# The last routed layer of a transformer block in three float32r products instead of float32 matmuls

## Chip, cores, metric

The kernel runs on one core of a Trainium2 chip. A core has TensorE (PE, matrix products; PEld is its weight load), VectorE (DVE), ScalarE (ACT), GpSimd (POOL) and SyncE (SP), which issues the transfers. The metric is the device time of one execution in microseconds. Each engine works off its own queue in order; engines wait for each other by semaphores.

## The reference, cut to what matters

```python
x = x + attn_a(layernorm(x))      # x is (8, 512, 256) float32
x = x + ffn(layernorm(x))
x = x + attn_b(layernorm(x))      # gated linear attention, then a SwiGLU
x = x + ffn(layernorm(x))         # the layer that changes; same weights as the second line

def ffn(x):                       # 4096 tokens of 256 channels, 16 blocks of 64 hidden units
    prob = softmax(x @ router_w.T + router_b)
    mask = the 4 largest of the 16 blocks, token by token
    h = relu((x @ w1.T + b1) * mask_of_the_block)      # 1024 hidden units
    return h @ w2.T + b2
```

The router chooses four blocks by their rank, so the layers before it are computed in float32; the kernel computes all hidden units of all tokens and masks.

## The kernel before, in words

The residual stream stays in SBUF (`xres`, batches by slices of 128 positions). After the first attention, the rest is done for four slices k of 8 x 128 = 1024 tokens: a routed layer, linear attention (`gla`), a SwiGLU and a second routed layer. The order of the work is written out by hand at the end of `block_kernel` (lines 1411 to 1450): `between` (L904) runs a list of matmul units and, between them, steps of generators (`pieces`) that make the next stages ready on the other engines. A scheduling layer then orders each engine's queue, within what the code's tiles and buffers allow; a tile that reuses a buffer waits for the buffer's last readers.

`route(k, key)` (L990) normalizes a slice, turns it with TensorE into channels by tokens (`xnT`, two halves g of 512 tokens), adds the bias b2 to `xres` on GpSimd (L1000), computes the router and writes the mask. The mask goes to DRAM (`md`) and comes back spread over 64 partitions each (`mk`, four transfers of 256 KB, L1070), all on SP's queue. For the last layer, slices 0 and 1 are routed during swiglu(2) and swiglu(3), slices 2 and 3 during the last layer's own slices 0 and 1.

`routed_ffn(k, key, last)` (L1113) computes a half of 512 tokens at a time. For each of the 8 rows of 128 hidden units, two float32 matmuls with 512 columns (L1118) go into a PSUM bank, ScalarE (L1126) or, in the last layer for odd rows, VectorE (L1124) adds b1 and applies ReLU, and VectorE multiplies by the mask (L1127). Then `down` (L1083) takes two batches at a time: 2 x 8 matmuls of 256 columns (L1092), with 128 tokens of h as the loaded operand, and VectorE adds the result to `xres` (L1103, at the very end L1100). In the last layer each `xres` of 256 KB is then stored. `swiglu(k)` (L1140) has the same shape with other weights.

PSUM has four banks for hidden units (`ps_h`, L886), two for outputs (`ps_y`) and two for the routing and attention pieces (`ps_l`).

Weights: the routed layers' w1 and w2, the linear attention's projections (`q_w`, `q_wo` and smaller ones, L852 to L882) and the SwiGLU's weights (L883 to L885) are all loaded in this order on SP's queue, ahead of the out-projection (`out_projection`, L972, from `outC`), in the pool `wpool`. After the out-projection the pool that held `outC` is closed (L1412) and a pool `rest` opened in its space for the linear attention's tiles.

The type `HALF` is float32r, another reading of the same 32 bits. The first attention already uses it: queries are split in an upper and a lower part (`qh`, `ql`), and each part is a float32r matmul (L582, L608). The changed functions and what calls them:

Of the kernel before, what the change touches and what calls it, by code (L numbers as in the profile page):

```python
# [33 lines left out]
LN_EPS = 1e-5  # L34
RMS_EPS = 1e-6
REPL = -(2.0**127)
SENT = -(2.0**126)


@with_exitstack  # L40
def block_kernel(ctx: ExitStack, tc: tile.TileContext, t: dict, out: bass.AP):
    nc = tc.nc
# [6 lines left out]
    out_v = out.rearrange("b (k p) d -> p b k d", p=P)  # L49
# [57 lines left out]
    with ExitStack() as outer:  # L107
# [5 lines left out]
        def bank(name):  # L113
            return ps_e.tile([P, 512], F32, tag="e", name=name)
# [68 lines left out]
        with ExitStack() as inner:  # L183
# [7 lines left out]
                out=head_of, in_=head_of, compare_op=ALU.is_ge, fill=0.0,  # L191
# [3 lines left out]
                out=head_of, in_=head_of, compare_op=ALU.is_ge, fill=0.0,  # L195
# [456 lines left out]
            def top_queries():  # L652
# [28 lines left out]
            first = front(0, lambda name: next(both)(name), True)  # L681
# [56 lines left out]
            for n in range(len(steps) + LAG + 1):  # L738
# [3 lines left out]
                batch, i = divmod(n - LEAD, 16)  # L742
# [76 lines left out]
        wpool = ctx.enter_context(tc.tile_pool(name="wpool", bufs=1, side="right"))  # L819
# [3 lines left out]
        for h in range(2):  # L823
            nc.sync.dma_start(
                out=rw[:, :, h, bass.ts(h, NBLK)],
                in_=t["f_router_wT"].rearrange("(c p) e -> p c e", p=P),
            )
        rb = load_rows(wpool, "rb", t["L0_ffn_router_b"], nc.sync)
        w1 = load_chunked(wpool, "w1", t["f_w1T"], nc.sync)
        b1 = load(wpool, "b1", t["f_b1c"], nc.sync)  # L830
        w2 = load_chunked(wpool, "w2", t["f_w2T"], nc.sync)
        b2 = load_rows(wpool, "b2", t["L0_ffn_b2"], nc.sync)

        with tc.tile_pool(name="a_tail", bufs=2) as tail:
# [5 lines left out]
            last = outC[5][0:1, 1, 0:1]  # L840
# [8 lines left out]

    G4 = NB // 2  # L850

    q_w = wpool.tile([P, NC2, NC2, 4, P], F32, name="q_w")  # L852
    for i, name in enumerate(("b_wkT", "b_wqT", "b_wvT", "b_wogT")):
        for c in range(NC2):
            nc.sync.dma_start(
                out=q_w[:, c, :, i, :],
                in_=t[name][bass.ts(c, P), :].rearrange("p (m n) -> p m n", n=P),
            )
    q_wo = load_chunked(wpool, "q_wo", t["b_woT"], nc.sync)


    q_wg1 = wpool.tile([P, NC2, 32], F32, name="q_wg1")
    q_wg2 = wpool.tile([P, D], F32, name="q_wg2")
    q_bg1 = wpool.tile([P, 1], F32, name="q_bg1")
    gh = wpool.tile([P, 2 * P], F32, name="gh")
    for w in (q_wg1, q_wg2, q_bg1):
        nc.gpsimd.memset(w, 0.0)
    nc.gpsimd.memset(gh, 1.0)
    nc.sync.dma_start(
        out=q_wg1[:, :, 0:DH], in_=t["b_wg1T"].rearrange("(c p) e -> p c e", p=P)  # L870
    )
    for u in range(G4):
        r = 32 * u + DH
        nc.sync.dma_start(out=q_wg2[32 * u : r, :], in_=t["b_wg2T"])
        nc.sync.dma_start(
            out=q_wg2[r : r + 1, :].rearrange("o (c p) -> o c p", p=P),
            in_=t["b_bg2c"].rearrange("p c -> c p").unsqueeze(0),
        )
        nc.sync.dma_start(out=q_bg1[32 * u : r, :], in_=t["b_bg1c"])
    q_bog = load(wpool, "q_bog", t["b_bogc"], nc.sync)  # L880
    scale1 = load(wpool, "scale1", t["b_scale1c"], nc.sync)
    scale2 = load(wpool, "scale2", t["b_scale2c"], nc.sync)  # L882
    w_gate = load_chunked(wpool, "w_gate", t["b_w_gateT"], nc.sync)  # L883
    w_up = load_chunked(wpool, "w_up", t["b_w_upT"], nc.sync)
    w_down = load_chunked(wpool, "w_down", t["b_w_downT"], nc.sync)  # L885
# [6 lines left out]
    def bank_h(name):  # L892
        return ps_h.tile([P, 512], F32, tag="h", name=name)
# [10 lines left out]
    def between(units, pieces, n):  # L904

        done = 0
        for i, unit in enumerate(units):
            unit()
            while done < n * (i + 1) // len(units):
                next(pieces, None)  # L910
                done += 1
        for _ in pieces:
            pass

    def tokens(k, b, n=2):
        return xres[:, b : b + n, k, :]

    def pairs(y):
        return y.rearrange("p (b d) -> p b d", d=D)
# [67 lines left out]
    ready = {}  # L987
    ROUTE = 10
# [124 lines left out]
    def routed_ffn(k, key, last):  # L1113
        def unit(h, g, f):
            xT, mk = ready[key]
            ps = bank_h("h_ps")
            for c in range(NC2):
                nc.tensor.matmul(  # L1118
                    ps, w1[:, c, bass.ts(f, P)], xT[g][:, c, :],
                    start=(c == 0), stop=(c == NC2 - 1),  # L1120
                )
            hf = hidden()
            if last and f % 2:
                nc.vector.tensor_scalar(hf, ps, b1[:, f : f + 1], 0.0, ALU.add, ALU.max)  # L1124
            else:
                nc.scalar.activation(hf, ps, AF.Relu, bias=b1[:, f : f + 1])  # L1126
            nc.vector.tensor_tensor(hf, hf, mk[g][:, f, :], ALU.mult)  # L1127
            h.append(hf)
            newest[0] = hf[0:1, 0:1]

        units = []
        for g in range(2):
            h = []
            units += [functools.partial(unit, h, g, f) for f in range(NF)]
            for u in range(2):
                units += down(h, w2, k, g, u, last)
        return units


    def swiglu(k):  # L1140
        def unit(h, pg, g, f, w):
            zT = ready["z", k]
            ps = bank_h("swi_ps")
            for c in range(NC2):
                nc.tensor.matmul(  # L1145
                    ps, w[:, c, bass.ts(f, P)], zT[g][:, c, :],
                    start=(c == 0), stop=(c == NC2 - 1),
                )
            if w is w_gate:
                hf = hidden()  # L1150
                nc.scalar.activation(hf, ps, AF.Silu)  # L1151
# [12 lines left out]
        return units  # L1164
# [5 lines left out]
    def gla(k):  # L1170
# [186 lines left out]
        for b in range(0, NB, 2):  # L1357
            y = bank_l("gla_y")
            for i in range(2):
                for m in range(NC2):  # L1360
                    nc.tensor.matmul(  # L1361
                        y[:, bass.ts(i, D)], oT[:, b // G4, m, bass.ts(b % G4 + i, P)],
                        q_wo[:, m, :],
                        start=(m == 0), stop=(m == NC2 - 1),
                    )
            z = post.tile([P, 2, D], F32, tag="z", name="z", bufs=4)
# [36 lines left out]
    def chain(*gens):  # L1403
        return itertools.chain(*gens)
# [8 lines left out]
    rest = ctx.enter_context(tc.tile_pool(name="rest", bufs=1, reuse_waits="tile"))  # L1413

    bog = wpool.tile([P, NC2, P], F32, name="bog")
# [27 lines left out]
    between(routed_ffn(3, (1, 3), False), chain(g[1], some(g[2], 34)), GLA - 42)  # L1443
    between(swiglu(1), chain(g[2], some(g[3], 24)), GLA - 10)
    between(swiglu(2), chain(g[3], route(0, (2, 0))), GLA - 24 + ROUTE)
    between(swiglu(3), route(1, (2, 1)), ROUTE)
    between(routed_ffn(0, (2, 0), True), route(2, (2, 2)), ROUTE)
    between(routed_ffn(1, (2, 1), True), route(3, (2, 3)), ROUTE)
    for k in (2, 3):
        between(routed_ffn(k, (2, k), True), iter(()), 0)  # L1450


# [47 lines left out]
```

## Time and profile before

| what | us |
|---|---|
| median of three runs (1587.17, 1594.52, 1595.94) | 1594.52 |
| span of the profiled execution, first to last instruction | 1583.6 |
| median of the runs above that span | 10.9 |
| TensorE busy | 1536.1 (97%) |
| VectorE busy | 942.4 (60%) |
| ScalarE busy | 703.6 (44%) |
| GpSimd busy | 454.0 (29%) |

The profile shows one execution; its span lies inside the time that the runs measure. Its page gives the engines' busy times, then the span in 40 slices, the chain of work that ended last, and groups of instructions: line, engine, operation, tile written and tiles read, shape, number, then busy time and mean duration, then the idle time before them and what ended it. The timeline view lists instructions in order of time: start, length, engine, line, operation, tiles, number of them. Busy times of matmuls overlap, since they are pipelined; their rate is read from the distance between starts.

### The profile page before, as it was taken

Reading aid. Unit: us, or ns where it says so; the run is one execution under the profiler, and the core shown is the slowest. Engines: PE = TensorE matmul, PEld = TensorE weight load, DVE = VectorE, ACT = ScalarE, POOL = GpSimd, SP = SyncE. Lnnn points to the kernel's source line nnn. Section 1 sums busy time; section 2 is a strip of 40 time slices with the busy share of each in tenths; the row PEclk is TensorE's granted clock in tenths of the full one; section 3 lists DMA queues with packets and bytes.
Section 4 is the critical chain, followed back from the end, with each engine's and each line's share of the span. In section 5 each row is a group of like instructions: output and inputs, shape, how many; then the busy total and the mean of one; then the engine's idle time right before and its main releaser. Section 6 shows DMA issues by size and latency. Waiting matters only on the chain.

```text
span 1583.6 us, 21546 instructions
## 1 busy us (share of the span) xinstructions
PE 1536.1 (97%) x7982; PEld 858.6 (54%) x7982; DVE 942.4 (60%) x1974; ACT 703.6 (44%) x1290; POOL 454.0 (29%) x547
## 2 busy tenths in 40 slices
PE   6899999999999899999899999999999999999999
PEld 3444444444444466655565556546545655667666
DVE  5888776776788864456834556567176532354332
ACT  4477777677778543532254225332631532211110
POOL 4743352452221241232433223334143310100000
PEclk9899999999999899999999999999999999999999
DMA  5301112112110330100000000000000010001100
GB/s 190 124 26 59 42 46 79 42 42 82 42 42 3 92 102 9 42 1 14 0 1 0 0 25 4 0 0 1 1 1 1 1 28 1 27 28 46 35 27 27
DMA packets 38553, 52.65 MB, mean 33 GB/s; under 512 B 9068, under 2 KB 22580, under 8 KB 38448
## 3 DMA queue, kind: packets, MB, share of 16 engines
q1 hardware_dynamic: 37648, 50.09, 9.8%
q8 instruction: 63, 1.03, 0.3%
q10 hardware_dynamic: 800, 1.18, 0.2%
q14 instruction: 42, 0.34, 0.1%
HBM read 21.24 MB, written 4.33 MB: 16 GB/s over the span
## 4 chain that ended last, share of the span: by engine, by line
PE 74%; DVE 11%; POOL 5%; ACT 4%; issue 3%; DMA 2%; SPq 0%; POOLq 0%; DVEq 0%; ACTq 0%
PE y_ps L1092 16%; PE h_ps L1118 10%; PE s L608 9%; PE swi_ps L1145 8%; PE av L630 7%; PE proj_ps L1231 7%; PE s L582 4%; DVE pr L1264 2%; PE q_ps L440 2%; POOL o L1281 2%; DVE pr L1254 2%; PE k_ps L440 2%; PE gla_y L1361 2%; PE v_ps L507 2%; DVE w L1256 2%
## 5 line engine op out<-in xcount | busy, mean ns | idle before, releaser
L588 DVE TENSOR_REDUCE mx<-s 128x1 f32<-128x512 f32 x512 | 325.3, 684 | 108.8 <-PE s L582 107.7
L615 ACT ACTIVATE e<-s 128x512 f32<-128x512 f32 x512 | 275.9, 600 | 119.5 <-PE s L608 115.0
L1092 PE MATMUL y_ps<-w,h 128*128 128x256 f32 x1024 | 232.9, 383 | 8.7 <-DVE h L1127 8.1
L1118 PE MATMUL h_ps<-xnT,w 128*128 128x512 f32 x512 | 228.2, 594 | 0.0
L1092 PEld LDWEIGHTS y_ps<-w,h 128*128 128x128 f32 x1024 | 193.2, 191 | 47.1 <-DVE h L1127 12.0
L1118 PEld LDWEIGHTS h_ps<-xnT,w 128*128 128x128 f32 x512 | 94.7, 190 | 105.8 <-issue 104.1
L630 PE MATMUL av<-e,va 128*32 128x512 f32 (+1 forms) x1216 | 144.4, 543 | 2.0 <-ACT st L640 2.0
L1126 ACT ACTIVATE h<-h_ps,b 128x512 f32<-128x512 f32 x96 | 65.3, 685 | 176.7 <-PE h_ps L1118 176.7
L1127 DVE TENSOR_TENSOR h<-h,mk 128x512 f32<-128x512 f32 x128 | 94.0, 748 | 80.4 <-ACT h L1126 60.7
L582 PE MATMUL s<-km,qh 32*128 32x512 f32 x512 | 135.6, 501 | 5.8 <-DMA km<-half 4.1
L608 PE MATMUL s<-qh,km 32*128 32x512 f32 x512 | 138.6, 499 | 0.4 <-ACT e L615 0.3
L1103 DVE TENSOR_TENSOR xres<-xres,y_ps 128x512 f32<-128x512 f32 x47 | 32.2, 685 | 154.4 <-PE y_ps L1092 117.2
L1145 PE MATMUL swi_ps<-zT,w_up 128*128 128x512 f32 x256 | 121.7, 594 | 0.2 <-DVE h L1154 0.2
L1145 PE MATMUL swi_ps<-zT,w_gate 128*128 128x512 f32 x256 | 121.4, 593 | 0.0
L1092 PE MATMUL y_ps<-w_down,h 128*128 128x256 f32 x512 | 117.6, 380 | 0.0
L1231 PE MATMUL proj_ps<-q_w,rT 128*128 128x512 f32 x256 | 115.7, 595 | 0.9 <-ACT al L1214 0.4
L608 PE MATMUL s<-ql,km 32*128 32x512 f32 x512 | 111.2, 400 | 0.0
L582 PE MATMUL s<-km,ql 32*128 32x512 f32 x512 | 109.5, 404 | 0.0
L608 PE MATMUL s<-tops,takes 4*128 4x512 f32 x512 | 109.0, 394 | 0.0
L582 PEld LDWEIGHTS s<-km,qh 32*128 32x128 f32 x512 | 54.4, 184 | 96.1 <-DVE mx L588 64.4
L1092 PEld LDWEIGHTS y_ps<-w_down,h 128*128 128x128 f32 x512 | 95.1, 190 | 19.0 <-issue 7.4
L1151 ACT ACTIVATE h<-swi_ps 128x512 f32<-128x512 f32 x64 | 38.1, 595 | 139.7 <-PE swi_ps L1145 139.6
(235 smaller groups left out, 2186.9 us busy)
## 6 DMA issues: line engine op xcount, KB each, us to landing
mk<-md SPq DMA_DIRECT2D x32, 256.0 KB
qh<-half SPq DMA_DIRECT2D x63, 128.0 KB
ql<-half SPq DMA_DIRECT2D x63, 128.0 KB
km<-half SPq DMA_DIRECT2D x63, 128.0 KB
out<-xres SPq DMA_DIRECT2D x15, 256.0 KB
xres<-in_L_attn_a_x SPq DMA_DIRECT2D x7, 512.0 KB
w<-in_f_w1T SPq DMA_DIRECT2D x1, 1024.0 KB
w<-in_f_w2T SPq DMA_DIRECT2D x1, 1024.0 KB
```

What stands on the lines that cost most here:

```text
L440: nc.tensor.matmul(ps, w[:, c, bass.ts(m, P)], x[:, c, :], start=(c == 0), stop=(c == NC2 - 1),)
L582: nc.tensor.matmul(s, (qh, ql)[i].bitcast(HALF)[rows, e, bass.ts(k, P)], km.bitcast(HALF)[rows, e, :], start=(i == 0), stop=(i == 1),)
L588: nc.vector.tensor_reduce(mx[:, b % 2, m, e, r : r + 1], s, AX.X, ALU.max)
L608: nc.tensor.matmul(s, keys.bitcast(HALF), queries.bitcast(HALF), start=(i == 0), stop=(i == 2),)
L615: nc.scalar.activation(ex, s, AF.Exp, scale=1.0 / DH**0.5)
L630: nc.tensor.matmul(av[32 * j : 32 * j + 32, queries], va[:, 8 * kt + 4 * m + j, DH * e : DH * e + 2 * DH], es[j][:, queries], start=(kt == ...
L1092: nc.tensor.matmul(y[0][:, bass.ts(i, D)], h[f][:, bass.ts(2 * u + i, P)], w[:, f, :], start=(f == 0), stop=(f == NF - 1),)
L1118: nc.tensor.matmul(ps, w1[:, c, bass.ts(f, P)], xT[g][:, c, :], start=(c == 0), stop=(c == NC2 - 1),)
L1126: nc.scalar.activation(hf, ps, AF.Relu, bias=b1[:, f : f + 1])
L1127: nc.vector.tensor_tensor(hf, hf, mk[g][:, f, :], ALU.mult)
L1145: nc.tensor.matmul(ps, w[:, c, bass.ts(f, P)], zT[g][:, c, :], start=(c == 0), stop=(c == NC2 - 1),)
L1231: nc.tensor.matmul(ps, rT[b // G4][:, c, bass.ts(b % G4, P)], q_w[:, c, m], start=(c == 0), stop=(c == NC2 - 1),)
```

## The change

The last routed layer gets its own code. In place of one float32 matmul, each operand is parted in an upper part u of 12 bits, a lower part l and a third, d. Three float32r matmuls are run: u by u and l by l into one PSUM sum y, and d by d into another, yd. The result is 4097 y - 4096 yd. The parts are made so that this gives all four products of upper and lower halves: for values, u is rounded by ScalarE with the scale 1 - 2^-13, l = x - u, and d = 4097/4096 u - x; the weights' u is held scaled by 2^-12.

- The weights are parted once, in eight pieces, during swiglu(3) (`part_weights`).
- The layer works in 16 groups of 256 tokens, each in four pairs of hidden rows. `up` has 12 matmuls of 256 columns for a pair; two ScalarE operations read yd with the bias, VectorE adds 4097 y (L1529 of the new code) and applies ReLU and mask (L1530), and `part_values` parts the hidden values: u on ScalarE (L1481), l on GpSimd (L1482), d on VectorE (L1483). `add_down` follows two pairs later with 12 matmuls; after a group's fourth pair, ScalarE, VectorE and GpSimd (L1557 to L1559) join its two sums and add them to `xres`, which is stored.
- The space for the parts comes from closing the pool `rest` after swiglu(2). So that it is large enough, `q_w`, `q_wo`, the smaller linear attention weights, `bog` and `z` move into `rest`; their loads and clearings are written after the out-projection and no longer ahead of it.

```diff
+NEAR = 1.0 - 2.0**-13
+DOWN = 2.0**-12
+BOTH = 4097.0
+LESS = -4096.0
...
-    q_w = wpool.tile([P, NC2, NC2, 4, P], F32, name="q_w")
...
+    resting = ctx.enter_context(ExitStack())
+    rest = resting.enter_context(tc.tile_pool(name="rest", bufs=1, reuse_waits="tile"))
+
+    q_w = rest.tile([P, NC2, NC2, 4, P], F32, name="q_w")
...
-    between(swiglu(3), route(1, (2, 1)), ROUTE)
-    between(routed_ffn(0, (2, 0), True), route(2, (2, 2)), ROUTE)
-    between(routed_ffn(1, (2, 1), True), route(3, (2, 3)), ROUTE)
-    for k in (2, 3):
-        between(routed_ffn(k, (2, k), True), iter(()), 0)
+    resting.close()
...
+    def part_weights(w, ws):
...
+            nc.scalar.activation(u, x, AF.Copy, scale=NEAR * DOWN)
+            yield
+            nc.vector.scalar_tensor_tensor(
+                l, ws[0][at], -1.0 / DOWN, x, ALU.mult, ALU.add
+            )
+            nc.vector.tensor_tensor(d, ws[0][at], ws[1][at], ALU.subtract)
+            yield
+
+    def part_values(x, to, eng):
+
+        u, l, d = to
+        nc.scalar.activation(u.bitcast(HALF), x, AF.Copy, scale=NEAR)
+        eng.tensor_tensor(l.bitcast(HALF), x, u, ALU.subtract)
+        nc.vector.scalar_tensor_tensor(
+            d.bitcast(HALF), u, 1.0 + DOWN, x, ALU.mult, ALU.subtract
+        )
+
+    def product(y, yd, w, x, first, last, **how):
+
+        for i in range(2):
+            nc.tensor.matmul(
+                y, w[i].bitcast(HALF), x[i].bitcast(HALF), start=first and i == 0,
+                stop=last and i == 1, **how,
+            )
+        nc.tensor.matmul(
+            yd, w[2].bitcast(HALF), x[2].bitcast(HALF), start=first, stop=last, **how
+        )
...
+    def up(n, p):
+        k, g = groups[n]
+        _, mk = ready[2, k]
+        y, yd = bank_h("h_ps"), bank_h("hd_ps")
+        for i in range(2):
+            f = 2 * p + i
+            for c in range(NC2):
+                product(
+                    y[:, bass.ts(i, W)], yd[:, bass.ts(i, W)],
+                    [w[:, c, bass.ts(f, P)] for w in w1s], [x[:, c, :] for x in xs[n]],
+                    c == 0, c == NC2 - 1,
+                )
+        h = parts.tile([P, 2, W], F32, tag="hf", name="hf", bufs=3)
+        for i in range(2):
+            f = 2 * p + i
+            nc.scalar.activation(
+                h[:, i, :], yd[:, bass.ts(i, W)], AF.Identity, bias=b1[:, f : f + 1], scale=LESS
+            )
+        flat = h.rearrange("p f t -> p (f t)")
+        nc.vector.scalar_tensor_tensor(flat, y, BOTH, flat, ALU.mult, ALU.add)
+        nc.vector.scalar_tensor_tensor(
+            h, h, 0.0, mk[g // 2][:, 2 * p : 2 * p + 2, bass.ts(g % 2, W)], ALU.max, ALU.mult
+        )
...
+        part_values(h, parted, nc.gpsimd)
+        hs[n, p] = parted
+
+    def add_down(n, p):
+        k, g = groups[n]
+        if p == 0:
+            bank = bank_l if n > 10 and n % 2 else bank_y
+            ys[n] = bank("y_ps"), bank("yd_ps")
...
+        if p == PAIRS - 1:
+            x = tokens(k, 2 * g)
+            t = parts.tile([P, L], F32, tag="hf", name="t", bufs=3)
+            nc.scalar.mul(t, yd, LESS)
+            nc.vector.scalar_tensor_tensor(t, y, BOTH, t, ALU.mult, ALU.add)
+            nc.gpsimd.tensor_tensor(x, x, pairs(t), ALU.add)
+            nc.sync.dma_start(out=out_v[:, 2 * g : 2 * g + 2, k, :], in_=x)
...
+        def unit(i):
+            if i < len(steps):
+                n, p = steps[i]
+                up(n, p)
+                if p == 1 and n + 1 < len(groups):
+                    part_inputs(n + 1)
+            if i >= LAGS:
+                add_down(*steps[i - LAGS])
...
+    between(
+        swiglu(3), chain(part_weights(w1, w1s), part_weights(w2, w2s), route(1, (2, 1))),
+        16 + ROUTE,
+    )
+    part_inputs(0)
+    units = last_ffn()
+    between(units[:20], route(2, (2, 2)), ROUTE)
+    between(units[20:42], route(3, (2, 3)), ROUTE)
+    between(units[42:], iter(()), 0)
```

More of the change, by code (lines that the diff above doesn't have):

```diff
@@ L850, in block_kernel @@
     G4 = NB // 2
-    q_w = wpool.tile([P, NC2, NC2, 4, P], F32, name="q_w")
[L853 to L882, printed above, removed]
     w_gate = load_chunked(wpool, "w_gate", t["b_w_gateT"], nc.sync)
@@ L1365, in gla @@
                     )
-            z = post.tile([P, 2, D], F32, tag="z", name="z", bufs=4)
+            z = rest.tile([P, 2, D], F32, tag="z", name="z", bufs=4)
             for i in range(2):
@@ L1412, in block_kernel @@
     outs.close()
-    rest = ctx.enter_context(tc.tile_pool(name="rest", bufs=1, reuse_waits="tile"))
-    bog = wpool.tile([P, NC2, P], F32, name="bog")
+    resting = ctx.enter_context(ExitStack())
+    rest = resting.enter_context(tc.tile_pool(name="rest", bufs=1, reuse_waits="tile"))
+    q_w = rest.tile([P, NC2, NC2, 4, P], F32, name="q_w")
+    for i, name in enumerate(("b_wkT", "b_wqT", "b_wvT", "b_wogT")):
+        for c in range(NC2):
+            nc.sync.dma_start(
+                out=q_w[:, c, :, i, :],
+                in_=t[name][bass.ts(c, P), :].rearrange("p (m n) -> p m n", n=P),
+            )
+    q_wo = load_chunked(rest, "q_wo", t["b_woT"], nc.sync)
+    q_wg1 = rest.tile([P, NC2, 32], F32, name="q_wg1")
+    q_wg2 = rest.tile([P, D], F32, name="q_wg2")
+    q_bg1 = rest.tile([P, 1], F32, name="q_bg1")
+    gh = rest.tile([P, 2 * P], F32, name="gh")
+    for w in (q_wg1, q_wg2, q_bg1):
+        nc.gpsimd.memset(w, 0.0)
+    nc.gpsimd.memset(gh, 1.0)
+    nc.sync.dma_start(
+        out=q_wg1[:, :, 0:DH], in_=t["b_wg1T"].rearrange("(c p) e -> p c e", p=P)
+    )
+    for u in range(G4):
+        r = 32 * u + DH
+        nc.sync.dma_start(out=q_wg2[32 * u : r, :], in_=t["b_wg2T"])
+        nc.sync.dma_start(
+            out=q_wg2[r : r + 1, :].rearrange("o (c p) -> o c p", p=P),
+            in_=t["b_bg2c"].rearrange("p c -> c p").unsqueeze(0),
+        )
+        nc.sync.dma_start(out=q_bg1[32 * u : r, :], in_=t["b_bg1c"])
+    q_bog = load(wpool, "q_bog", t["b_bogc"], nc.sync)
+    scale1 = load(wpool, "scale1", t["b_scale1c"], nc.sync)
+    scale2 = load(wpool, "scale2", t["b_scale2c"], nc.sync)
+    bog = rest.tile([P, NC2, P], F32, name="bog")
     ones = post.tile([P, P], F32, tag="row", name="ones", bufs=6)
@@ L1445, in block_kernel, with three @@
     between(swiglu(2), chain(g[3], route(0, (2, 0))), GLA - 24 + ROUTE)
-    between(swiglu(3), route(1, (2, 1)), ROUTE)
-    between(routed_ffn(0, (2, 0), True), route(2, (2, 2)), ROUTE)
-    between(routed_ffn(1, (2, 1), True), route(3, (2, 3)), ROUTE)
-    for k in (2, 3):
-        between(routed_ffn(k, (2, k), True), iter(()), 0)
+    resting.close()
+    parts = ctx.enter_context(tc.tile_pool(name="parts", bufs=1, reuse_waits="tile"))
+    def three(pool, shape, name, **how):
+        return [pool.tile(shape, F32, tag=f"{name}{i}", name=f"{name}{i}", **how) for i in "hld"]
@@ new lines, in block_kernel @@
+    w1s = three(parts, [P, NC2, DFF], "w1")
+    w2s = three(parts, [P, NF, D], "w2")
+    def part_weights(w, ws):
+        for i in range(4):
+            if w.shape[1] == NC2:
+                at = (slice(None), i // 2, bass.ts(i % 2, DFF // 2))
+            else:
+                at = (slice(None), bass.ts(i, NF // 4))
+            x, (u, l, d) = w[at], (y[at].bitcast(HALF) for y in ws)
+            nc.scalar.activation(u, x, AF.Copy, scale=NEAR * DOWN)
[5 more added lines that the diff above has]
+            yield
@@ new lines, in block_kernel, with part_inputs @@
+    PAIRS = NF // 2
+    LAGS = 2
+    W = 2 * P
+    groups = [(k, g) for k in range(4) for g in range(G4)]
+    xs, hs, ys = {}, {}, {}
+    def part_inputs(n):
+        k, g = groups[n]
+        xT, _ = ready[2, k]
+        xs[n] = three(parts, [P, NC2, W], "x", bufs=2)
+        part_values(xT[g // 2][:, :, bass.ts(g % 2, W)], xs[n], nc.gpsimd)
+    def up(n, p):
[4 more added lines that the diff above has]
+            f = 2 * p + i
+            for c in range(NC2):
+                product(
[8 more added lines that the diff above has]
+                h[:, i, :], yd[:, bass.ts(i, W)], AF.Identity, bias=b1[:, f : f + 1], scale=LESS
+            )
+        flat = h.rearrange("p f t -> p (f t)")
+        nc.vector.scalar_tensor_tensor(flat, y, BOTH, flat, ALU.mult, ALU.add)
+        nc.vector.scalar_tensor_tensor(
+            h, h, 0.0, mk[g // 2][:, 2 * p : 2 * p + 2, bass.ts(g % 2, W)], ALU.max, ALU.mult
+        )
+        parted = [
+            post.tile([P, 2, W], F32, tag="h", name=f"h{i}", bufs=8) for i in "hl"
+        ] + [parts.tile([P, 2, W], F32, tag="hd", name="hd", bufs=3)]
+        part_values(h, parted, nc.gpsimd)
+        hs[n, p] = parted
@@ new lines, in add_down @@
+    def add_down(n, p):
+        k, g = groups[n]
+        if p == 0:
+            bank = bank_l if n > 10 and n % 2 else bank_y
+            ys[n] = bank("y_ps"), bank("yd_ps")
+        y, yd = ys[n]
+        for i in range(2):
+            for j in range(2):
+                f = 2 * p + j
+                product(
+                    y[:, bass.ts(i, D)], yd[:, bass.ts(i, D)],
+                    [x[:, j, bass.ts(i, P)] for x in hs[n, p]], [w[:, f, :] for w in w2s],
+                    p == 0 and i == 0 and j == 0, p == PAIRS - 1 and i == 1 and j == 1,
+                    skip_group_check=True,
+                )
+        if p == PAIRS - 1:
[5 more added lines that the diff above has]
+            nc.sync.dma_start(out=out_v[:, 2 * g : 2 * g + 2, k, :], in_=x)
@@ new lines, in last_ffn @@
+    def last_ffn():
+        steps = [(n, p) for n in range(len(groups)) for p in range(PAIRS)]
+        def unit(i):
[6 more added lines that the diff above has]
+                add_down(*steps[i - LAGS])
+        return [functools.partial(unit, i) for i in range(len(steps) + LAGS)]
+    between(
+        swiglu(3), chain(part_weights(w1, w1s), part_weights(w2, w2s), route(1, (2, 1))),
+        16 + ROUTE,
+    )
```

## The prediction

> **What bounds the kernel now.** I read first the page's busy shares: TensorE 97% of 1583.6 us. Second the chain of work that ended last, for the stage that changes; its columns are start, length and what.
>
> ```profile
> 1469.48 13.73 PE h_ps L1118 x32
> 1483.21 13.81 PE y_ps L1092 x64
> 1497.03 13.73 PE h_ps L1118 x32
> 1510.76 13.81 PE y_ps L1092 x64
> ...
> 1580.53 0.02 issue
> 1580.56 0.42 DVE xres L1100
> ```
>
> The last routed layer is TensorE without a gap. A float32 matmul leaves two records here (L1118 has 512 for 256 matmuls): 512 columns take 2 x 0.429 us, 256 columns 2 x 0.216. The layer runs from 1352.7, where swiglu(3) hands over, to VectorE's last add at 1580.98: 228.3 us. Third the busy times of the stretch 1352.7 to 1583.6 (columns: length, then TensorE, weight loads, VectorE, ScalarE, GpSimd):
>
> ```profile
> 1352.70:1583.60 230.90, 227.24 (x870) 150.54 (x868) 92.08 (x190) 33.84 (x56) 6.27 (x5) 1.00 0.11 33
> ```
>
> Only TensorE is full; GpSimd is nearly idle. The change fills exactly these engines, so fourth the rate of a float32r product, from the attention's timeline, and fifth what VectorE and GpSimd do to each other.
>
> ```profile
> 502.59 0.51 PE L608 MATMUL s<-qh,km 32*128 32x512 f32 x4
> 502.93 0.40 PE L608 MATMUL s<-ql,km 32*128 32x512 f32 x4
> 503.15 0.41 PE L608 MATMUL s<-tops,takes 4*128 4x512 f32 x4
> ```
>
> Starts of two rounds of 512 columns lie 0.22 us apart (0.93 to 1.15): a quarter of 0.858.
>
> ```profile
> 1383.64 2.49 POOL L1000 TENSOR_TENSOR xres<-xres,b 128x512 f32<-128x512 f32 x2 [8.73 <-ACT row L939]
> 1385.15 1.53 DVE L1127 TENSOR_TENSOR h<-h,mk 128x512 f32<-128x512 f32 x1 [2.58 <-ACT h L1126]
> ```
> ```profile
> 924.76 2.49 DVE L1264 TENSOR_TENSOR pr<-made,w 128x512 f32<-128x512 f32 x4
> 925.59 4.48 POOL L1281 TENSOR_TENSOR o<-o,pr 128x512 f32<-128x512 f32 x2 [5.28 <-DVE pr L1264]
> 927.16 0.69 DVE L1103 TENSOR_TENSOR xres<-xres,y_ps 128x512 f32<-128x512 f32 x1
> 927.76 1.18 DVE L1326 TENSOR_TENSOR pr<-pr 128x512 f32<-128x512 f32 x1
> ```
>
> A VectorE operation with both inputs in SBUF and a GpSimd operation exclude each other. L1127, alone 0.69, ends 0.55 after GpSimd's end (1386.13). GpSimd's first L1281 waits until the row of L1264 is through (927.25) and ends 1.13 later (2.80 us in all, where L1000 takes 1.27 alone); L1326 then ends 0.55 after it. L1103, with one input in PSUM, is not touched. Where both wait, VectorE went first, and back to back it keeps the port.
>
> **The change on TensorE.** Removed: 128 matmuls of 512 columns and 256 of 256: 128 x 0.858 + 256 x 0.432 = 220.3 us (the other 8 us are the routing of slices 2 and 3, and the end). Added: 64 pairs (16 groups x 4) x 24 float32r matmuls of 256 columns = 1536. No row has one with 128 rows and a fresh 128x128 load each. Low end 0.11 (half of 0.22); high end 0.20, with a load not hidden (L1092 shows 0.309 instead of 0.216 between starts where its load had to wait: 0.093). I take 0.11, since L1092's loads hide behind 0.216 and transposes run at 0.109 with a load each: 2.64 us a pair, 10.5 a group against 13.8, 169 us in all. By TensorE alone that is 51 us less.
>
> On loads the Trainium skill ("TensorE: Matmul & The Clock Gate", section "LDWEIGHTS (loading the stationary operand)") gives columns divided by 1.2 ns, 107 ns here; an estimate by that page's warm gap, 256/2.4 + 2.5, is 109 ns a matmul, so a load would just hide; no run shown has this shape.
>
> **The change on the other engines, per pair.** ScalarE: two Identity of 256 columns from PSUM (L1126's 0.69 less 0.20, the step between L179 and L525: 0.50, starts 0.40 apart) and one Copy, U (0.60, L179 with 0.59). VectorE: A (L1529, one input in PSUM, 0.69 like L1103), M (L1530, ReLU and mask, both inputs in SBUF, 0.69 like L1127), S (L1483, both in SBUF, 0.69 like L148). GpSimd: L (L1482, 1.28, L455). Per group: one more U, S and L for the inputs (XU, XS, XL), one ScalarE mul and VectorE T at the end, and GpSimd's ADD. Hand-over ScalarE to VectorE is 0.03 (1451.02 to 1451.05), to GpSimd 0.08 (588.36 to 588.45).
>
> The ring is A, M, U, S of one pair, then A of the next. Without GpSimd: S 0.60 (the next can start), A and M 0.69 + 0.03 each, U 0.60 + 0.03, together 2.67, beside TensorE's 2.64. With GpSimd the port decides. One group without routing, in the built order, us from S of pair 0: S0 0.69; L0 1.82 (beside it A1 and T, no port); M1 2.50; ADD 3.63; S1, whose U was ready at 3.2, 4.18; M2 4.78; L1 5.90; XS 6.45; S2 7.06; XL 8.18; M3 8.73; L2 9.85; S3 10.40; L3 11.53; M of the next group's pair 0 12.08. Its U stands in ScalarE's queue behind the first Identity of the pair after; that needs an up-projection which TensorE has behind a down-projection waiting for L3, so S0' comes at **13.6**, not 12.7. Six GpSimd turns of 1.13 (6.8), nine of VectorE (5.3), and 1.5 of hand-over. Bounds: 12.1 (no hand-over) and 15.2 (all serial: four times L, S, A, M, U and hand-overs, 1.28 + 0.55 + 0.65 + 0.65 + 0.60 + 0.07). I take 13.6, the order as built. So TensorE's 3.3 us a group are given back: its 10.5 wait on a ring of 13.6, and before it was 13.8.
>
> Of the port, the Trainium skill ("SBUF — State Buffer", section "Who interferes with whom") says that a VectorE instruction with two SBUF inputs and a GpSimd instruction that reads SBUF block each other, whichever issues first; it speaks against putting L on GpSimd. It has one instruction as the unit; the row of L1264 shows GpSimd waiting through several. If GpSimd came in after each single one, L1 would end some 0.6 us earlier, an estimate of up to 9 us less over the layer.
>
> **The sum.** Start, until the first U is done: 12 x 0.11 + 0.2 + 0.40 + 0.50 + 0.69 + 0.69 + 0.60 + 0.1 = 4.5. 63 further pairs, 15.75 x 13.6 - 1.8 (the last group has no XS, XL) = 212.4. Routing of slices 2 and 3: five L1000 (5 x 1.13) and about 9.5 us of VectorE operations, until now hidden under TensorE; between 0 and 15, I take the middle, 7.5. End: S and L 1.9, rest of the down-projection 1.2, mul, T and ADD 2.6, hand-overs 0.3 = 6.0. Together 230.4 against 228.3: +2.1. The last store is 256 KB, not 128: +0.3 (0 to 0.8).
>
> Parting the weights: 8 U and 16 VectorE operations (11 us) inside swiglu(3), where VectorE is busy 26.3 of 86.7 us: hidden, 0; without that cover, 11.
>
> The q_w loads move behind the out-projection, because their space is freed there, and 9 large and 4 small of them now stand in SP's queue before the masks of slice 0. Now:
>
> ```profile
> 589.72 2.43 SPq L1070 DMA_DIRECT2D mk<-md  x4
> 594.52 4.31 DVE L1127 TENSOR_TENSOR h<-h,mk 128x512 f32<-128x512 f32 x7 [6.82 <-DMA mk<-md]
> ```
>
> They can issue from 583.4 (the last out-projection add), some 0.7 us each as now; md goes at about 590 instead of 587.07, the masks at 592.7, so L1127 starts 3.0 later. TensorE wants the products at 597.8 and has them at 597.0: 2.2 us late (0 to 6). Of the tiles that move pool, bog, gh and z, none issues more than before: 0.
>
> Total +2.1 + 0.3 + 2.2 = +4.6 on the span of 1583.6. The median of the times shown, 1594.5, lies 10.9 above that span, so I predict 1583.6 + 4.6 + 10.9 = **1599.1**.
>
> **Rivals.** (B) The port overlaps better: 12.1 to 13.0 a group, -19 to -5 us, 1575 to 1590. For it: 1.5 us a group are hand-over only. Against: the queues are in order. (C) GpSimd first: if L gets the port before S after each U, every pair becomes the serial chain, 15.2 a group, 15.75 x 1.6 = +25, about 1624, slower. It decides once S is ready over 0.05 us later than L (0.08 less 0.03), as when VectorE is still in A. Against: VectorE's hand-over is shorter. (D) No exclusion for these operations, so that the change does what it says: TensorE and the ring without GpSimd bind, 10.7 to 11.9 a group, about -30, some 1564. Against: L1127's 1.53. (E) Loads not hidden: 24 x 0.20 = 4.8 a pair, 307 us, about +90, 1685.
>
> **How the numbers follow.** (A) 13.0 to 14.2 a group: 0.44, from 1589 to 1608; B 0.27; C, with all of 14.2 to 15.2, 0.20; D 0.05; E 0.04. Under 0.5% (8 us) no measurement here tells a difference. Faster: B's 0.22 beyond it and D, 0.27. Within: 0.05 of B and 0.31 of A, 0.36. Slower: 0.13 of A, C, E: 0.37. The range takes A, B and the lower half of C: 1575 to 1617, and leaves out 0.19.
>
> **What would show it.** L1490 and L1494 at 0.11 us between starts (E: 0.20). TensorE idle a fifth of the layer, waiting for L1482 and L1483. M, S and XS of over 1 us beside GpSimd (none: D). Groups 13.6 us apart after the last routing. S before L after each U (else C). L1127 at 597.5 in slice 0. Wrong would be above all a ring that isn't set by the port, or a layer far from 230 us.

## The result, and the profile after

The changed kernel took 1617.3 us (median of four runs, 1610.5 to 1618.9), the kernel before 1590.9 beside it on the same chip: ratio 1.0157, 95% interval 1.0116 to 1.0197. It is 1.6% slower. The forecast was 1599.1 with a range from 1575 to 1617: the side is right, the time lies at the very end of the range, and it is missed by 18 us. As a change the miss is larger: 4.6 us were forecast, less than the 8 us that the prediction took to be measurable, and the two medians lie 26.5 us apart. The profiled execution (1610.53) has a span of 1608.8, 25.2 more than the span of 1583.6 before.

First the stretch of the last layer, from its first product to the end of the span. The columns are the length, then TensorE, weight loads, VectorE, ScalarE, GpSimd, the granted clock, the DMA share and GB/s. Before, it was 230.9 long with TensorE busy for 227.24.

```profile
1360.90:1608.80 247.90, 209.78 (x1638) 194.31 (x1636) 205.59 (x299) 117.41 (x246) 165.73 (x99) 0.98 0.10 31
```

TensorE is no longer full: it is busy for 17.5 us less, and the stretch is 17 us longer. VectorE and GpSimd, nearly idle here before, are busy for most of it. What TensorE waits for, from the view of waits for the same stretch (total, times, longest):

```profile
PE y_ps L1490 <- POOL hl L1482: 26.5, 39, 2.3
PE yd_ps L1494 <- DVE t L1558: 2.8, 3, 1.5
PE yd_ps L1494 <- DVE hd L1483: 1.9, 7, 0.9
```

It waits for L, GpSimd's lower part of the hidden values (A, M, U, S, L, XU, XS, XL, T and ADD are the prediction's names for the operations of a pair and a group). The chain of waits within one group (start, length, what) has no TensorE in it, where before it was nothing else:

```profile
1550.63 0.69 DVE hf L1529
1551.32 0.69 DVE hd L1483
1552.01 0.78 DVE hf L1530
1552.79 0.84 issue
1553.63 1.59 DVE xd L1483
...
1555.34 1.78 DVE hd L1483
```

XS and S (L1483) stand in it with 1.59 and 1.78 us, where 0.69 is their length alone. The timeline of the same stretch, GpSimd's and VectorE's rows and one of ScalarE's, shows M (L1530) at 1.78 too, and why:

```profile
1547.82 0.69 DVE L1483 SCALAR_TENSOR_TENSOR hd<-hh,hf 128x512 fp32r<-128x512 f32 x1 [0.76 <-ACT hh L1481]
...
1549.79 1.67 POOL L1559 TENSOR_TENSOR xres<-xres,t 128x512 f32<-128x512 f32 x1
...
1551.24 0.77 DVE L1483 SCALAR_TENSOR_TENSOR hd<-hh,hf 128x512 fp32r<-128x512 f32 x1
1551.42 1.74 POOL L1482 TENSOR_TENSOR hl<-hf,hh 128x512 fp32r<-128x512 f32 x1
1551.93 1.78 DVE L1530 SCALAR_TENSOR_TENSOR hf<-hf,mk 128x512 f32<-128x512 f32 x1
...
1553.24 1.62 POOL L1482 TENSOR_TENSOR xl<-xnT,xh 128x512 fp32r<-128x512 f32 x1
1553.63 1.78 DVE L1483 SCALAR_TENSOR_TENSOR xd<-xh,xnT 128x512 fp32r<-128x512 f32 x1
...
1554.82 1.74 POOL L1482 TENSOR_TENSOR hl<-hf,hh 128x512 fp32r<-128x512 f32 x1
1555.34 1.78 DVE L1483 SCALAR_TENSOR_TENSOR hd<-hh,hf 128x512 fp32r<-128x512 f32 x1
...
1559.20 0.69 DVE L1483 SCALAR_TENSOR_TENSOR hd<-hh,hf 128x512 fp32r<-128x512 f32 x1 [0.76 <-ACT hh L1481]
...
1560.53 1.04 DVE L1530 SCALAR_TENSOR_TENSOR hf<-hf,mk 128x512 f32<-128x512 f32 x1
1561.67 0.63 ACT L1481 ACTIVATE hh<-hf 128x512 fp32r<-128x512 f32 x1 [1.04 <-DVE hf L1530]
1562.33 0.69 DVE L1483 SCALAR_TENSOR_TENSOR hd<-hh,hf 128x512 fp32r<-128x512 f32 x1 [0.76 <-ACT hh L1481]
...
1565.74 0.79 DVE L1483 SCALAR_TENSOR_TENSOR hd<-hh,hf 128x512 fp32r<-128x512 f32 x1
```

Add start and length of each: from the second row on, the ends are 1551.46 (ADD), 1552.01 (S), 1553.16 (L), 1553.71 (M), 1554.86 (XL), 1555.41 (XS), 1556.56 (L), 1557.12 (S). The two engines take turns, one operation each: VectorE ends 0.55 after GpSimd, GpSimd 1.15 after VectorE. M starts in its queue at 1551.93, while S still runs, and yet L goes between them. That is the row on which the prediction fell: it had M follow S and L come after both.

The groups' ends (L1559) lie 14.5 us apart where nothing else runs, against 13.6 in the prediction. The first ten of these distances, beside the routing of slices 2 and 3, are 151.9 us together, 6.9 more than ten times 14.5.

TensorE's own rate, from its timeline (start, length, engine, line):

```profile
1561.42 0.28 PE L1490 MATMUL y_ps<-w2h,hh 128*128 128x256 f32 x1
1561.53 0.28 PE L1490 MATMUL y_ps<-w2l,hl 128*128 128x256 f32 x1
1561.65 0.28 PE L1494 MATMUL yd_ps<-w2d,hd 128*128 128x256 f32 x1
```

Starts are 0.11 to 0.12 apart (median 0.118 over the layer), each with a fresh 128x128 load: the loads hide, and 96 products are 11.3 us a group.

Two smaller costs lie ahead of the layer. On SP's queue the moved loads stand before the masks, as predicted (rows of SP's queue):

```profile
589.61 0.60 SPq L86 DMA_DIRECT2D q_wo<-in_b_woT  x1
590.31 0.86 SPq L1038 DMA_DIRECT2D md<-mT  x1
...
594.05 2.44 SPq L1043 DMA_DIRECT2D mk<-md  x4
```

And in swiglu(3), where VectorE now parts the weights too, TensorE waits for a mask that VectorE finishes later; before, it waited for nothing there. The second row is VectorE's: an operation that parts the weights, with 1.74 us where others of its line take 0.68, stands in the queue directly before the mask's last steps (L1018, then L1026).

```profile
PE mT_ps L1033 <- DVE taken L1026: 1.7, 1, 1.7
```
```profile
1282.73 1.74 DVE L1475 TENSOR_TENSOR w2d<-w2h,w2l 128x512 fp32r<-128x512 f32 x1
```

### The profile page after: what moved, and what is told of

It reads as the page before. It is cut to its first block, busy times and chain, and to the rows that moved or that the text cites. A ratio compares the mean times of both kernels' runs of the same rounds, so it can differ in the third digit from the quotient of the medians.

```text
span 1608.8 us, 23764 instructions
## 1 busy us (share of the span) xinstructions
PE 1522.9 (95%) x8750; PEld 901.3 (56%) x8750; DVE 1070.2 (67%) x2101; ACT 792.6 (49%) x1490; POOL 615.8 (38%) x643
## 4 chain that ended last, share of the span: by engine, by line
PE 59%; DVE 21%; ACT 7%; POOL 6%; issue 5%; DMA 2%; SPq 0%; POOLq 0%; ACTq 0%; DVEq 0%
PE s L612 10%; PE y_ps L1065 9%; PE av L634 8%; PE swi_ps L1118 7%; PE proj_ps L1204 7%; PE s L586 4%; PE h_ps L1091 3%; DVE hf L1530 3%; DVE pr L1237 2%; DVE hf L1529 2%; DVE pr L1227 2%; PE q_ps L444 2%; DVE hd L1483 2%; PE k_ps L444 2%; PE gla_y L1334 2%
## 5 line engine op out<-in xcount | busy, mean ns | idle before, releaser
L634 PE MATMUL av<-e,va 128*32 128x512 f32 (+1 forms) x1216 | 148.5, 558 | 2.1 <-ACT st L644 2.0
L1482 POOL TENSOR_TENSOR hl<-hf,hh 128x512 fp32r<-128x512 f32 x64 | 110.0, 1720 | 76.3 <-ACT hh L1481 67.9
L1065 PE MATMUL y_ps<-w,h 128*128 128x256 f32 x512 | 122.9, 391 | 8.8 <-DVE h L1100 8.6
L1091 PE MATMUL h_ps<-xnT,w 128*128 128x512 f32 x256 | 115.9, 594 | 0.0
L1065 PEld LDWEIGHTS y_ps<-w,h 128*128 128x128 f32 x512 | 96.6, 194 | 32.9 <-DVE h L1100 14.7
L1490 PE MATMUL y_ps<-w2l,hl 128*128 128x256 f32 x256 | 78.4, 306 | 27.2 <-POOL hl L1482 26.5
L612 PEld LDWEIGHTS s<-qh,km 32*128 32x128 f32 x512 | 57.0, 187 | 75.7 <-ACT e L619 52.2
L973 POOL TENSOR_TENSOR xres<-xres,b 128x512 f32<-128x512 f32 x32 | 43.4, 1376 | 121.5 <-ACT row L912 112.7
```

Source lines behind the costliest of these rows:

```text
L612: nc.tensor.matmul(s, keys.bitcast(HALF), queries.bitcast(HALF), start=(i == 0), stop=(i == 2),)
L634: nc.tensor.matmul(av[32 * j : 32 * j + 32, queries], va[:, 8 * kt + 4 * m + j, DH * e : DH * e + 2 * DH], es[j][:, queries], start=(kt == ...
L1065: nc.tensor.matmul(y[0][:, bass.ts(i, D)], h[f][:, bass.ts(2 * u + i, P)], w[:, f, :], start=(f == 0), stop=(f == NF - 1),)
L1091: nc.tensor.matmul(ps, w1[:, c, bass.ts(f, P)], xT[g][:, c, :], start=(c == 0), stop=(c == NC2 - 1),)
L1482: eng.tensor_tensor(l.bitcast(HALF), x, u, ALU.subtract)
L1490: nc.tensor.matmul(y, w[i].bitcast(HALF), x[i].bitcast(HALF), start=first and i == 0, stop=last and i == 1, **how,)
```

## The experiments

All but before_2 start from the changed kernel, and each ratio is to the kernel before on the same chip. The first product of the last layer falls anywhere from 1357 to 1372 us in the profiles of these variants, so single profiles are compared by stages. The medians were taken on several chips, so two variants are compared by their ratios and layers. "Layer" is the stretch from the layer's first product to the end of the span, "group" the distance between the ends of groups past the last routing.

| kernel | median us | ratio to before (95%) | layer | group |
|---|---|---|---|---|
| changed | 1617.3 | 1.0157 (1.0116 to 1.0197) | 247.9 | 14.5 |
| m_psum | 1591.4 | 0.9994 (0.9970 to 1.0017) | 226.8 | 13.05 |
| no_l | 1580.8 | 0.9923 (0.9897 to 0.9948) | 214.0 | 11.97 |
| pipe | 1614.3 | 1.0147 (1.0105 to 1.0189) | 251.5 | 14.52 |
| pipe_m | 1581.8 | 0.9902 (0.9868 to 0.9937) | 217.6 | 12.03 |
| pipe_m_tail | 1586.6 | 0.9941 (0.9911 to 0.9971) | 216.5 | 12.0 |
| best2 | 1582.8 | 0.9951 (0.9932 to 0.9970) | 218.2 | 12.03 |
| s_halves | 1643.4 (one run) | | 284.3 | 16.77 |
| loads_late | 1617.0 (one run) | | 247.8 | 14.5 |
| early | 1615.2 (one run) | | 247.6 | 14.5 |
| before, before_2 | | | 230.9, 230.9 | |

**m_psum: M out of the port**

```diff
-nc.vector.scalar_tensor_tensor(flat, y, BOTH, flat, ALU.mult, ALU.add)
+nc.vector.scalar_tensor_tensor(y, y, BOTH, flat, ALU.mult, ALU.add)
 nc.vector.scalar_tensor_tensor(
-    h, h, 0.0, mk[...], ALU.max, ALU.mult
+    h, y.rearrange("p (f t) -> p f t", t=W), 0.0, mk[...], ALU.max, ALU.mult
```

> One edit to the changed kernel: VectorE's A leaves its result in the PSUM bank of y, and M reads it from there, so that M has only one input in SBUF. Theory (port taken in turns): in the changed kernel VectorE's operations with two SBUF inputs and GpSimd's take turns one by one, 0.55 us and 1.15 us a turn, and that makes a group 14.5 us instead of the 13.6 of the prediction. Then M falls from 1033 to some 690 ns, the row of S, L, M, XL, XS, L, S loses two turns, and a group takes 12.2 to 13.0 us; the layer loses 22 to 35 us, the whole some 1588. Rival 1 (ring through ScalarE): U, then both Identity operations of the next pair, A, M set the pace, 0.62 + 0.90 + 0.71 + 0.70 = 2.93 a pair, and the port adds only M's 0.35: then the gain is at most 4 x 0.35 = 1.4 us a group, 13.1 or more, the whole 1597 or more. Rival 2 (TensorE, 0.118 a matmul, or its loads): no change.

21 us came off the layer and 26 off the median, with the same operations on the same engines. M in the groups view from 1476 us on (number, busy, mean ns), of the changed kernel and of m_psum:

```profile
L1530 DVE SCALAR_TENSOR_TENSOR hf<-hf,mk 128x512 f32<-128x512 f32 x27 | 27.9, 1034 | 0.4
```
```profile
L1530 DVE SCALAR_TENSOR_TENSOR hf<-h_ps,mk 128x512 f32<-128x512 f32 x26 | 17.8, 686 | 1.0
```

With one input in PSUM, M no longer waits at the port, and rival 2's "no change" falls. Between the theory and rival 1 this run doesn't decide. The median is below rival 1's 1597, but the group is 13.05, just above the theory's 12.2 to 13.0 and within 0.1 of rival 1's 13.1, and the layer's 21 us lie below the theory's 22 to 35. Rival 1 is decided by the next two kernels.

**no_l: GpSimd's L left out**

```diff
-part_values(h, parted, nc.gpsimd)      # u, l, d of the hidden values
+part_values(h, parted, None)           # u and d; l is one unchanging tile
```

> The lower parts of the hidden values are left out: GpSimd's L of each pair isn't computed, and TensorE reads one unchanging tile in their place, as often as before. GpSimd keeps XL and ADD, two turns a group instead of six. Theory (port taken in turns): without L, M and S are 0.69 nearly everywhere, the group falls to 11.8 to 12.5 us, the layer by 32 to 43 us, the whole to some 1580. What is left above TensorE's 24 x 4 x 0.118 = 11.3 is the ring without port. Rival 1 (ring through ScalarE, 2.93 a pair): 11.7 plus 0.6 for XU, 12.3 at the least, and TensorE still idle between pairs. Rival 2 (TensorE sets the layer): unchanged, 14.5.

As the theory said, 1580.8. TensorE is busy 47.03 of 48 us past the routing, so what is left is nearly all TensorE's own. The group is 11.97, under the 12.3 that rival 1 needs at the least. Leaving L out takes away its turns at the port and also TensorE's wait for L; this run alone can't tell the two apart.

**pipe: another order, the same port**

```diff
 up(n, p)                     # products and two Identity
+if i:
+    finish(*steps[i - 1])    # A, M, U, L, S of the pair before
...
-LAGS = 2
+LAGS = 3
```

> Only the order in which the code hands out the work is changed: a pair's products and its two Identity operations come first, then A, M, U, L, S of the pair before, and the down-projection follows three pairs later instead of two (hd with four buffers instead of three). All operations stay as they are, and so do the port's turns. On ScalarE the Identity operations of the next pair then stand before U. Theory (port taken in turns): six GpSimd turns of 1.15 and the VectorE turns between them remain, 12 to 12.5 us at the least, and what goes is the stretch in which the chain waits outside the port; a group at 12.5 to 13.5 us, the whole about 1590 to 1602. Rival 1 (ring through ScalarE): the Identity operations leave the ring, so a pair falls to about TensorE's 2.83, a group to 11.4 to 11.8, the whole to 1575 or less. Rival 2 (TensorE): unchanged.

Rival 1 falls: the Identity operations left the ring, and the group stays at 14.52. But the theory's own number fell too (1590 to 1602 expected, 1614 measured). Its timeline shows what it had not seen:

```profile
1565.12 0.63 ACT L1481 ACTIVATE hh<-hf 128x512 fp32r<-128x512 f32 x1 [2.52 <-DVE hf L1536]
...
1565.79 0.69 DVE L1483 SCALAR_TENSOR_TENSOR hd<-hh,hf 128x512 fp32r<-128x512 f32 x1 [0.76 <-ACT hh L1481]
1565.89 1.73 POOL L1482 TENSOR_TENSOR hl<-hf,hh 128x512 fp32r<-128x512 f32 x1 [1.41 <-ACT hh L1481]
...
1567.29 0.87 DVE L1536 SCALAR_TENSOR_TENSOR hf<-hf,mk 128x512 f32<-128x512 f32 x1
...
1568.26 0.63 ACT L1481 ACTIVATE hh<-hf 128x512 fp32r<-128x512 f32 x1 [1.78 <-DVE hf L1536]
...
1568.92 0.69 DVE L1483 SCALAR_TENSOR_TENSOR hd<-hh,hf 128x512 fp32r<-128x512 f32 x1 [0.76 <-ACT hh L1481]
```

This is a ring through the port. S ends at 1566.48, L 1.14 later (1567.62), M of the next pair 0.54 after L (1568.16), then U, and S again 3.13 us after the S before. The port doesn't only add its turns: by way of L it ties each pair's M to the pair before. In pipe's steady group three of the four steps from S to S are 3.13 to 3.16, and the fourth, with XL, XS and ADD, is 5.10: 14.52 in all.

In the changed kernel the ring is there, but it isn't all. The ends of S in the rows further up (1552.01, 1557.12, 1559.89, 1563.02, 1566.53) are 5.11, 2.77, 3.13 and 3.51 apart. The first step is the port's turns L, M, XL, XS and L; the second is A, M, U and S without a wait at the port; the third is the ring; in the fourth, S stands behind the next A in VectorE's queue and behind ADD at the port. That both kernels come to 14.52 from different steps is not explained. pipe_m and pipe_m_tail were made on the theory of the ring.

**pipe_m: both edits**

> Both edits together: the order of pipe (products and Identity of a pair ahead of A, M, U, L, S of the pair before) and M read from PSUM as in m_psum. Theory now (a ring through the port): a pair takes 3.13 us because M of the next pair stands behind L at the port, U behind M, S behind U and L behind S (0.55 + 0.71 + 0.68 + 1.15 = 3.1), with or without the Identity operations; XL, XS and ADD add 2.0 to a group, 14.5. That is why pipe alone brought nothing. With M out of the port the ring is open; what held m_psum at 13.05 was U, Identity, A, M of the next pair, and the new order takes that away too. So a group comes near TensorE's 96 x 0.118 = 11.3, 11.3 to 12.2, and the whole to 1568 to 1582. Rival 1: the two edits don't add up, since another queue (S and XS behind L and XL at the port, or ScalarE's) holds a group at 12.8 or more: the whole within 6 us of m_psum. Rival 2: the bank of y is now held until M is through and TensorE waits for it: slower than m_psum.

Alone, the order brought nothing (layer 251.5 against 247.9); with M out of the port it brings 9 us more (217.6 against 226.8). TensorE past the routing, first of the changed kernel, then of pipe_m:

```profile
1522.00:1570.00 48.00, 42.26 (x323) 39.05 (x322) 42.28 (x47) 22.72 (x47) 34.85 (x22) 1.00 0.15 45
```
```profile
1522.00:1570.00 48.00, 47.12 (x393) 46.59 (x392) 39.75 (x56) 26.04 (x55) 39.25 (x24) 1.00 0.11 34
```

393 products against 323 in the same time: TensorE is the bound again. Group and time are as expected, at the upper end, and both rivals fall. This kernel beats the one before by 1% (0.9868 to 0.9937).

**pipe_m_tail: a turn of the port less**

```diff
-nc.scalar.mul(t, yd, LESS)
-nc.vector.scalar_tensor_tensor(t, y, BOTH, t, ALU.mult, ALU.add)
-nc.gpsimd.tensor_tensor(x, x, pairs(t), ALU.add)
+nc.vector.scalar_tensor_tensor(x, pairs(yd), LESS, x, ALU.mult, ALU.add)
+nc.vector.scalar_tensor_tensor(x, pairs(y), BOTH, x, ALU.mult, ALU.add)
```

> As pipe_m, and the end of each group is done by VectorE from PSUM: x = -4096 yd + x, then x = 4097 y + x; ScalarE's mul, VectorE's T and GpSimd's ADD go. One turn of the port and one GpSimd operation less in a group, one VectorE operation more. Theory (ring through the port): where the ring is open and TensorE sets the pace, a turn less is worth little, 0 to 0.5 us a group, 0 to 8 us in all. Rival 1 (port as a sum of turns): each GpSimd turn costs 1.15 + 0.55 wherever it stands, so 1.1 to 1.7 a group less, 17 to 27 us.

216.5 against 217.6: no gain that can be told, as expected. Rival 1, 17 us or more, falls: where TensorE sets the pace, a turn at the port costs nothing that can be told.

**s_halves: who gets the port**

```diff
-nc.vector.scalar_tensor_tensor(d, u, 1.0 + DOWN, x, ALU.mult, ALU.subtract)
+for i in range(2):           # 256 columns each, back to back, hidden values only
+    nc.vector.scalar_tensor_tensor(d[:, i, :], u[:, i, :], 1.0 + DOWN, h[:, i, :], ...)
```

> In the changed kernel S of the hidden values is issued as two operations of 256 columns, back to back, with no wait between them. It asks who gets the port. Theory (turns): L, whose wait ends 0.1 us after that of S, comes in after the first half and ends 1.15 later, and the second half ends some 0.3 after L. Rival (the rule of the prediction, from L1264: VectorE keeps the port from one operation to the next as long as nothing stands between them): L comes after both halves. The time says little either way: 1610 to 1630.

```profile
1567.45 1.84 DVE L1540 SCALAR_TENSOR_TENSOR hd<-hh,hf 128x256 fp32r<-128x256 f32 x2 [0.76 <-ACT hh L1537]
1567.56 1.45 POOL L1538 TENSOR_TENSOR hl<-hf,hh 128x512 fp32r<-128x512 f32 x1 [2.48 <-ACT hh L1537]
```

L ends at 1569.01, the second half of S only at 1569.29: L went between the halves, so the rule from L1264 doesn't hold here. The expectation on the time was wrong: 1643 instead of 1610 to 1630. A then waits for the second half, L stands in the ring of every pair, and the pairs come 3.93 us apart. Splitting one VectorE operation in two made the layer 36 us longer than in the changed kernel (284.3 against 247.9). The one execution took 33 us more than the changed kernel's profiled one (1643.4 against 1610.5), since it reached its last layer 3.5 us earlier.

**before_2: how much of the start belongs to the change**

> The kernel before, unchanged, for a second profile on the chip of these runs. The changed kernel reaches its last layer 8.2 us later in its profile than the kernel before. Theory: only some 2 us of that come from the change (first mask 4.4 us later, TensorE 2.0), the rest is the granted clock and the loads of that one execution; then this profile reaches its last layer 3 us or more away from 1352.7, or varies as much in its first 580 us. Rival: the 8.2 us belong to the change, and this profile is at 1352.7 within 1 us.

The unchanged kernel has its first routed product at 596.0 here and at 582.5 in the first profile, at a mean granted clock of 0.973 and 0.987. So the start varies by 13.5 us with nothing changed. From there to the last layer it takes 772.1 and 770.2, the changed kernel 776.8: 4.7 to 6.6 us do come with the change, more than the theory's 2 and less than the rival's 8.2.

**loads_late and early: ahead of the layer**

loads_late writes the moved loads after the routed layer of slice 0. early has them issued by GpSimd (`nc.gpsimd.dma_start`) and, in swiglu(3), parts w2 after the routing:

```diff
-chain(part_weights(w1, w1s), part_weights(w2, w2s), route(1, (2, 1)))
+chain(part_weights(w1, w1s), route(1, (2, 1)), part_weights(w2, w2s))
```

> In the changed kernel the loads of q_w, q_wo and q_wg1, q_wg2, q_bg1 are written after the routed layer of slice 0 instead of ahead of it; the last layer is as in the changed kernel. Counted from the first routed product, the kernel before has the first mask product at 12.0 and 12.3, the first swiglu at 232.2 and 233.8, the last layer at 770.2 and 772.1; the changed kernel and its variants 14.9 to 15.6, 235.5 to 237.2, 776.8 to 777.7. Theory: the masks of slice 0 wait behind the loads on SP's queue, and that is the 3 us up to the first swiglu; so the first mask comes at 12 to 12.5, the first swiglu at 233 to 234, the last layer at 774 to 775 (1.7 us stay, the transpose in swiglu(3) that waits for the mask behind the parting of the weights). Rival: the loads only change places with the masks, and the delay stays or moves to the linear attention, which needs the weights: the first swiglu at 235.5 or later.

> Two edits ahead of the last layer, which stays that of the changed kernel: the loads of q_w, q_wo and the small linear attention weights are issued by GpSimd instead of SP, and in swiglu(3) w2 is parted after the routing of slice 1 instead of before it. (In the run with the loads written later, SP's queue kept the old order, loads ahead of masks, so that run undid nothing.) Theory: the masks wait behind the loads on SP, and the mask transpose of swiglu(3) waits 1.7 us behind the parting of w2; so, counted from the first routed product, the first mask product comes at 12 to 12.5 (15 in the changed kernel), the first swiglu at 233 to 234.5 (235 to 237), and the stretch from the fourth swiglu to the last layer falls from 330.5 to 332 back to 328.6 to 329.2 counted from the second swiglu; the last layer at 772 to 774. Rival: the delay has another cause, or GpSimd's issuing costs as much: the first swiglu at 235.5 or later.

loads_late undid nothing: on SP's queue the loads still stood ahead of the masks, and the first mask product came 15.4 us after the first routed product. In early no load stands between them on SP's queue, and md issues 4.6 us after the first routed product, as before:

```profile
595.80 0.33 SPq L1038 DMA_DIRECT2D md<-mT  x1
599.36 2.42 SPq L1043 DMA_DIRECT2D mk<-md  x4
604.58 1.90 DVE L1100 TENSOR_TENSOR h<-h,mk 128x512 f32<-128x512 f32 x3 [8.15 <-DMA mk<-md]
```

The first mask product is 13.3 after the first routed product (before 12.0, changed 14.9, expected 12 to 12.5). At the first transposes behind the masks TensorE is 0.7 us later than before, where the changed kernel is 2.2. The first swiglu comes 232.2 after the first routed product (before 232.2, changed 236.6) and the last layer 774.5 (changed 776.8). These two hold less than they seem to: up to the first swiglu the granted clock was 0.99 here and 0.98 in the changed kernel, and best2, with the same two edits, doesn't repeat them (see there). The other edit brought nothing: TensorE waits 2.2 us for the mask transpose, instead of 1.7. In early the parts of w1 still stand among the router's steps in VectorE's queue, and no run takes them out too.

**best2: pipe_m and early together**

> pipe_m (M read from PSUM, products and Identity of a pair ahead of the rest of the pair before) together with the two edits of early. Theory: pipe_m's layer of 213 to 215 us, where TensorE is full from group 10 on (11.9 to 12.0 a group), less 2 to 5 us ahead of it: 1575 to 1581, 0.9 to 1.3 per cent under the kernel before. Rival: the edits ahead of the layer are lost in the waits of its first groups, where the routing of slices 2 and 3 runs: as pipe_m, 1579 to 1586.

The theory falls (1582.8 and a layer of 218.2 against 1575 to 1581 and 213 to 215), and the rival's "as pipe_m" stands. In this profile the first swiglu comes 238.0 us after the first routed product, at a granted clock of 0.97, and TensorE is 3.6 us later than before at the first transposes behind the masks, against 2.2 in the changed kernel. VectorE's and GpSimd's rows there:

```profile
609.62 2.70 DVE L1100 TENSOR_TENSOR h<-h,mk 128x512 f32<-128x512 f32 x1
609.98 0.49 POOL L1416 DMA_DIRECT2D q_bg<-in_b_bg1c  x1
610.49 1.27 POOL L973 TENSOR_TENSOR xres<-xres,b 128x512 f32<-128x512 f32 x1
```

GpSimd's add of the bias stands behind the loads that GpSimd now issues: it comes 19.9 us after the first routed product, in the changed kernel 5.9. Here it met a mask product, which ended 0.56 after it and took 2.70 us instead of 0.68, and TensorE waited 2.5 us. In early the same add began 0.6 us after that mask product had ended. So the edit that freed the masks can bring a collision at the port, and whether it is worth anything is not shown. What held the mask product between 609.62 and the add's start at 610.49 is not shown either.

The intervals of pipe_m, pipe_m_tail and best2 all lie under 1, so the form of product that this change brings does beat float32 here, by half to one per cent, once M is out of the port and the order is changed.

## Why the prediction was right or wrong

The span was forecast 4.6 us longer and is 25.2 us longer. Of the 20.6 us between, the layer gives 14.6 (predicted 230.4 + 2.6 + 0.3 = 233.3, measured 247.9), and its later start 6.0 (2.2 and 8.2). The distance from 1599.1 to 1617.3 is only 18.2, since the median lies 8.5 above the profiled span and not 10.9; that 2.4 comes of which execution was profiled, not of the change.

- **The step that failed**: "Where both wait, VectorE went first, and back to back it keeps the port." In the group's table it put M2 ahead of L1. The rows from 1547.82 on (S0) agree with the table until S1 (4.19 after the start of S0, predicted 4.18). Then it goes L 5.34, M 5.89, XL 7.04, XS 7.59, L 8.74, S 9.30, where the table had S2 end at 7.06, and the next group starts at 14.5, not 13.6. 0.9 x 15.75 = 14.2 us, nearly all that the layer was off. But 0.9 is what two errors leave. The table also had the next group's U wait behind an Identity, S0' at 13.6 "not 12.7"; in the rows M ends at 1561.57 and U starts at 1561.67, waiting for M alone. With 12.7 the layer would have been some 28 us off (1.8 x 15.75), so that it was only 14.6 is partly luck. s_halves shows the same order from another side. Why GpSimd had waited through three of L1264's operations was not tried and stays open. The rule that the prediction took from the Trainium skill ("SBUF — State Buffer", section "Who interferes with whom"), with one instruction as the unit, holds in these rows. But the estimate worked out from it, up to 9 us less, had the wrong sign: a GpSimd operation that comes in earlier holds up M and S, on which the next pair waits.
- **The forms of the rivals**: the group fell in C's band (14.2 to 15.2) by another mechanism. Pairs are not serial, and S still goes before L. B falls (14.5 a group, not 12.1 to 13.0). E falls (0.118 a product) and D (M 1034 ns beside GpSimd, 686 out of the port).
- **The ring**: A, M, U, S without GpSimd, 2.67 in the prediction, is one of the four steps of a group (2.77). The prediction didn't draw the ring M, U, S, L by way of the port: 3.13 in another step, and in three of four once pipe had changed the order.
- **TensorE**: 0.118 a product instead of 0.11, and of no weight, as it waited.
- **Right**: start to the first U 4.8 (4.5), routing 6.9 (7.5), end 6.2 (6.0), last store 3.1 instead of 2.6 (0.3 more predicted), the masks 2.9 later (3.0) and TensorE 2.2 late (2.2).
- **Parting the weights, "hidden, 0"**: wrong by 1.7, the wait for the mask in swiglu(3), if the parts that stand before the mask in VectorE's queue are its cause; the rows show the order, and no run shows the wait gone. VectorE had the time, but not in the stretch in which the router needed it. Of the 8.2 us of later start, 2.2 and 1.7 are so accounted for, and 1.6 lie ahead of the first routed product, where the changed kernel only has loads and clearings less; 2.7 stay open, and before_2 differs from before by 1.9 in that stretch with nothing changed.

## What to carry to other kernels

When work moves to GpSimd, transfers that it issues included, mark each VectorE operation with two SBUF inputs and draw the ring with turns of one operation each; a GpSimd operation costs where it ties one pair to the next, not by its length. Giving such a VectorE operation one input in PSUM took it out of the port and was worth 21 us of the layer, and an order that brought nothing before brought 9 us after it. Where the start of a program varies by 14 us, compare stages.

## What the runs showed of the hardware

- A float32r product of 256 columns with a fresh 128x128 load takes 0.11 to 0.12 us from start to start (median 0.118), so its load hides. The Trainium skill's page "TensorE: Matmul & The Clock Gate", section "LDWEIGHTS (loading the stationary operand)", gives columns divided by 1.2 ns, an estimate of 107 ns for such a load; that fits under 0.118.
- Two VectorE operations of 256 columns cost more than one of 512 beside a waiting GpSimd operation: it gets its turn between them (1.84 us from start to end instead of 0.69).
- The 22 loads moved from SP to GpSimd for issue cost GpSimd some 17 us of busy time (82.6 against 65.5 from the first routed product to the first swiglu), and GpSimd's next add stands behind them.
